# A two-layer graph-attention kernel: projection and gate of layer 0 as one product of fifteen block products

## The chip, the cores and the metric

The kernel runs on one core of one Trainium2 chip. The metric is device time in microseconds (us) for one execution, the median of the runs; the profile is one execution taken by the hardware profiler. TensorE (PE in the profile, its weight loads PEld) multiplies matrices and writes to PSUM, eight banks of 128 x 512 float32. VectorE (DVE), ScalarE (ACT) and GpSimd (POOL) do the elementwise work; SyncE (SP) issues all DMAs of this kernel from one queue.

## The reference

128 graphs of 64 nodes with 768 features go through two layers, each followed by a residual and a layer norm. Cut to what matters:

```python
def _L0_gnn_ref(feat_in, adj, W, b, w_src, w_dst, H_w, H_b):
    h = jnp.einsum('bnd,ade->bane', feat_in, W)          # 12 heads of 64
    th = jnp.tanh(h)
    attn = einsum(th, w_src) + swapaxes(einsum(th, w_dst), 2, 3)
    attn = jnp.where(attn >= 0, attn, 0.2 * attn)
    attn = softmax(jnp.where(~adj, -999.0, attn), axis=-1)
    feat_out = elu(attn @ h + b)
    gate = jax.nn.sigmoid(feat_in @ H_w.T + H_b)
    return gate * feat_out + (1.0 - gate) * feat_in

x = _layernorm(x + _L0_gnn_ref(x, adj, ...))
x = _layernorm(x + _L1_gnn_ref(x, ...))   # q, k, v projections, 6 heads, masked softmax, output projection
```

All arithmetic is in float32. The change lies in layer 0, and in the places of weights that layer 1 finds there.

## The kernel before

A tile is 128 rows (two graphs), a pair is two tiles; there are 32 pairs (`NP`). Layer 0 runs over the pairs one turn after the other, layer 1 then over 16 groups of two pairs. The order of every engine's work is written out by hand (`manual_schedule`), nothing reorders it.

**Block products.** A projection of a pair (256 rows by 768 by 768) is not taken as eight block products of a 2 x 2 split but as seven, in Strassen's manner. `Job` (L247) names them 1 to 7: each is three matmuls (`HK`) of 128 rows by 384 columns (`HALF`), line L270. Four operands are sums of input blocks (`block_sums`, L232), four weight blocks are sums too (`weight_sums`, L213). Products 1, 6, 7 and 4 pile up in one PSUM bank `y`, 2 has a bank `x`, 5 and 3 share `z`; between two products on one bank the partial result is drained: `way_out` (L279) copies it on ScalarE where a result is first written, and adds it on VectorE elsewhere (h: L850 to L852, gate: L866 to L868, values of layer 1: L879 to L881). In each turn three jobs run: `h` and `gate` of pair p, and the values `v` of layer 1 for pair p - 1, whose products 4 and 3 fall in the next turn, under the name `u`. `step` (L305) issues a product and then the drain of the product before it. Layer 1 uses a larger scheme of fifteen products of a 3 x 2 split for q, k and the output (`WIDE`, L70).

**The attention of layer 0**, per tile t (t1 and t0 are the second and the first of a pair): `products` (L884) takes tanh(h) and multiplies it with w_dst on VectorE and w_src on GpSimd; `terms` (L893) reduces both on VectorE into `sd` (128 x 24), writes the first twelve columns, the neighbour terms, to DRAM (`dstd`, L899) and reads them back as rows that all 64 nodes of a graph see (`dd`, L902); `logits` (L922) adds them (L926), `leaky` (ScalarE, L936), `masked` (three VectorE instructions, L942 to L949), `exps` (ScalarE, L955), `probs_by_nodes` (TensorE transposes), `attend` (TensorE, L987), `features` (VectorE L1003 and L1004, ScalarE exponential L1011), `elu1`, `gated` (L1022 to L1029), `stats` and `normed` (layer norm), `by_features` (transposes into `x1T`, operand of the values). `gate_tanh` (ScalarE) and `residual` (GpSimd, L1017) work on the gate.

**The order of a turn.** `TURN` (L121) lists the products; a plan hangs other work behind positions of that list: `at` for pair p, `was` for pair p - 1.

```python
TURN = [
    "h1", "h2", "u4", "u3", "h6", "g1", "h5", "h7", "g2", "g6", "h4",
    "h3", "g5", "g7", "v1", "v2", "g4", "v6", "g3", "v5", "v7",
]
```

In it `terms` of t1 and t0 hang at positions 13 and 14 and `logits` at 16 and 18 of the same turn; `masked` of t1 and t0 at 18 and 20. What lies past the end of the list is carried into the next turn. A DMA that waits for data holds up the DMAs behind it on SP's queue.

Of the kernel before, what the change touches and what calls it, by code (L numbers as in the profile page):

```python
# [24 lines left out]
EP = E0 + 2  # L25
# [21 lines left out]
WOVEN = [  # L47
    (0, 1), (1, 1), (0, 2), (1, 2), (0, 6), (1, 6), (0, 5),
    (0, 7), (1, 5), (1, 7), (0, 4), (0, 3), (1, 4), (1, 3),
]  # L50

FIRST = ["h1", "h2", "h5", "h6", "g1", "h7", "g2", "h4", "g6", "g5", "g7", "h3", "g3"]

FIRST_AT = {3: 0, 6: 10, 8: 3, 11: 8, 12: 12, 13: 12, 14: 13, 15: 14, 16: 14, 17: 14, 18: 15, 19: 19, 20: 19}
SECOND = [
    "h1", "G4", "h2", "g1", "g2", "h6", "h5", "h7", "g6", "h4",
    "g5", "g7", "h3", "g4", "g3", "H1", "v1", "v2", "v6", "v5", "v7", "H2",
]  # L60
SECOND_AT = {11: 10, 12: 13, 13: 13, 14: 14, 15: 14, 16: 15, 17: 16, 18: 18, 19: 19, 20: 20}
SECOND_OLD = {
    7.5: 12, 0: 7, 1: 8, 2: 8, 3: 9, 4: 10, 5: 11, 6: 12, 7: 12, 8: 13, 9: 14, 11: 15, 12: 15, 15: 16, 16: 17, 19: 19,
}

# [26 lines left out]
    ["u4", "u3"]  # L95
    + [f"q{n}" for n in (0, 1, 2, 3, 4, 5, 6, 8, 7, 9, 10, 11, 12)]
    + ["v1", "v2", "v6", "q13", "v5", "v7", "q14", "v4", "v3"]
)
LAST_AT = {7.5: 8, 3: 3, 4: 4, 5: 5, 6: 6, 7: 7, 8: 9, 9: 10, 11: 12, 12: 13, 15: 15, 16: 17, 19: 18}
# [21 lines left out]
TURN = [  # L121
    "h1", "h2", "u4", "u3", "h6", "g1", "h5", "h7", "g2", "g6", "h4",
    "h3", "g5", "g7", "v1", "v2", "g4", "v6", "g3", "v5", "v7",
]

THIRD_AT = {pos: max(int(pos) - 2, 0) for pos in [*range(len(TURN)), 7.5]}
TURNS = {
    0: (FIRST, FIRST_AT, {}),
    1: (SECOND, SECOND_AT, SECOND_OLD),
    2: (TURN[2:], THIRD_AT, THIRD_AT),  # L130
}
# [3 lines left out]
def kernel(  # L135
# [9 lines left out]
    hwT: bass.AP,  # L145
# [33 lines left out]
    dst_d = [dram.tile([P, H0], F32, name=f"dstd_{t}") for t in range(2 * NP)]  # L179
# [199 lines left out]
    def wide_place(key, n):  # L379
        flat = weights[key].rearrange("p b k f -> p (b k f)")  # L380
        at = PLACE[n] * 2 * W2
        return flat[:, at : at + 2 * W2].rearrange("p (k f) -> p k f", k=2)
# [373 lines left out]
    with ExitStack() as ph, ExitStack() as ph_r:  # L756
# [34 lines left out]
        xTs[0] = sbr.tile([P, KC, PAIR * P], F32, tag="xT", name="xT_0")  # L791
        w0_w = weights["q"] = wpool.tile([P, 7, HK, HALF], F32, tag="wa", name="w0_wq")
        for kh, blocks in ((0, (B11,)), (1, (B21, T3, B22))):
            rows = slice(kh * HK, (kh + 1) * HK)
            nc.sync.dma_start(out=xTs[0][:, rows, :], in_=xT[0][:, rows, :])
            for block in blocks:
                load_block(w0, w0_w, block)
        hb_bc = load_rows(sbr, hb, D, "hb_bc")
        b01_bc = load_rows(sb, b0, E0, "b01_bc")
        hw_w = weights["k"] = load_weight(hwT, "wb", "hw_wk", (B11, B21, T3, B22))  # L800
# [3 lines left out]
        A[0], x_steps = sums_of(G, sbr, "sx", xTs[0], "x0")  # L804
        all_of(x_steps)
        t1, t2, t4, t3 = weight_sums(V, w0_w)
        all_of((t1, t2, t3, t4))
# [21 lines left out]
        def new_h(t):  # L829
            h = sb.tile([P, H0, EP], F32, tag="h", name=f"h_{t}", bufs=3)  # L830
            G.memset(h[:, :, E0:], 1.0)
            return h

        h_of = per_tile("h", new_h)
        gate_of = per_tile("gate", lambda t: sb.tile([P, D], F32, tag="gate", name=f"gate_{t}", bufs=3))
        v_of = per_tile("v", lambda t: sb.tile([P, D], F32, tag="v", name=f"v_{t}"))


        def h_job(p):
            def at(m, n):  # L840
                return h_of(p, m)[:, n * J0 : (n + 1) * J0, :E0]

            def as_heads(b):
                return b.rearrange("p (j e) -> p j e", e=E0)

            return token_job(
                f"h{p}",
                A[p],
                w0_w,
                lambda mn, b: S.copy(at(*mn), as_heads(b)),  # L850
                lambda mn, b: V.tensor_tensor(at(*mn), as_heads(b), at(*mn), ALU.add),
                lambda b: S.copy(at(1, 0), as_heads(b)),  # L852
            )

        def gate_job(p):
            def at(m, n):
                return gate_of(p, m)[:, n * HALF : (n + 1) * HALF]

            def bias(n):
                return hb_bc[:, n * HALF : (n + 1) * HALF]  # L860

            return token_job(
                f"g{p}",
                A[p],
                hw_w,
                lambda mn, b: V.tensor_tensor(at(*mn), b, bias(mn[1]), ALU.add),  # L866
                lambda mn, b: V.tensor_tensor(at(*mn), b, at(*mn), ALU.add),
                lambda b: V.tensor_tensor(at(1, 0), b, bias(0), ALU.add),  # L868
            )
# [14 lines left out]
        def products(t):  # L884

            h = st[t]["h"]
            th = sbr.tile([P, 2, D], F32, tag="th", name=f"th_{t}")
            S.activation(th[:, 1, :].rearrange("p (a e) -> p a e", e=E0), h[:, :, :E0], AF.Tanh)
            V.tensor_tensor(th[:, 0, :], th[:, 1, :], wsd[:, 0, :], ALU.mult)  # L889
            G.tensor_tensor(th[:, 1, :], th[:, 1, :], wsd[:, 1, :], ALU.mult)  # L890
            st[t]["th"] = th

        def terms(t):  # L893

            th = st[t].pop("th")
            sd = small.tile([P, 2 * H0], F32, tag="sd", name=f"sd_{t}")
            V.tensor_reduce(sd, th.rearrange("p s (a e) -> p (s a) e", e=E0), AX.X, ALU.add)
            st[t]["sd"] = sd
            nc.sync.dma_start(out=dst_d[t], in_=sd[:, :H0])  # L899
            dd = work(f"dd_{t}")  # L900
            for g in range(2):
                nc.sync.dma_start(  # L902
                    out=dd[g * N : (g + 1) * N, :],
                    in_=dst_d[t][g * N : (g + 1) * N, :]
                    .rearrange("m a -> (m a)")
                    .partition_broadcast(N),
                )
            st[t]["dd"] = dd

        def with_bias(t):  # L910

            h = st[t]["h"]
# [9 lines left out]
        def logits(t):  # L922
# [5 lines left out]
                dd.rearrange("p (m a) -> p a m", a=H0),  # L928
                sd[:, H0:].unsqueeze(2).to_broadcast([P, H0, N]),
# [50 lines left out]
        def attend(t):  # L980
            pT, h, hx = st[t].pop("pT"), st[t].pop("h"), st[t].pop("hx")
# [32 lines left out]
        def residual(t):  # L1014

            xp = st[t]["x"]
            G.tensor_tensor(xp, st[t]["gate"], xp, ALU.mult)  # L1017
# [6 lines left out]
        def gated(t):  # L1024

            ex, gate, u = (st[t].pop(k) for k in ("ex", "gate", "x"))
            V.scalar_tensor_tensor(ex, gate, 4.0, ex, ALU.add, ALU.mult)
# [35 lines left out]

        def gate_tanh(t):

            gt = st[t]["gate"]
# [19 lines left out]
        def x_sums(p):  # L1086
            operands, steps = sums_of(G, sbr, "sx", xTs[p], f"x{p}")
            all_of(steps)
            A.setdefault(p, {}).update(operands)

        def third_begins():
            x = xTs[2]
            A[2] = {1: x[:, :HK, :P], 2: x[:, HK:, :P]}
            jobs["H"] = h_job(2)

# [10 lines left out]
        v_sums, carried = {}, {}  # L1106
        summing = sum_weights(sb)
        for p in range(NP + 1):
# [70 lines left out]
            if p == NP:  # L1179
                flush()  # L1180
                for act in plan.pop(0):
                    act()
# [179 lines left out]
```

## Time and profile before

| | |
|---|---|
| runs, us | 2878.41, 2883.49, 2881.39 (median 2881.39) |
| span of the profiled execution, us | 2888.2 |
| PE busy in it | 2840.2 us, 98% |
| DVE busy | 1924.9 us, 67% |
| ACT busy | 1061.2 us, 37% |
| POOL busy | 1303.5 us, 45% |
| mean granted clock of TensorE | 0.998 |

The span runs from the first to the last instruction. A busy share is an average over both layers; a matmul's end in the profile is modelled, so that the distance from start to start says more than the length of one record. Every float32 matmul of 128 rows leaves two records, so a product of three matmuls leaves six. What bounds a stage is read from what waits last in it; idle time of an engine that others wait for little costs nothing.

### The profile page before, as it was taken

The page shows a single profiled execution, that of the slowest core. Times are in us where ns is not written, and L with a number is a line of the kernel's source. Part 1 is how long each engine was busy: PE and PEld are TensorE (multiplying, and loading weights), DVE is VectorE, ACT ScalarE, POOL GpSimd, SP SyncE. Part 2 cuts the span into 40 slices and gives each one's busy share as a digit, 9 for nine tenths or more (in the row PEclk, how much of TensorE's full clock was granted, in tenths as well). Part 3 has the DMA queues.
Part 4 walks back from the last instruction along what each step waited for, and adds up shares of the span by engine and source line. Part 5 has one row for each costly group of instructions (what it writes and reads, how often), then busy time and mean ns, then how long its engine had stood idle before and what let it go on. Part 6 is the DMA issues. An engine that isn't in the chain of part 4 may idle for free.

```text
span 2888.2 us, 47874 instructions
## 1 busy us (share of the span) xinstructions
PE 2840.2 (98%) x18252; PEld 2075.9 (72%) x18252; DVE 1924.9 (67%) x3203; ACT 1061.2 (37%) x1896; POOL 1303.5 (45%) x1253
## 2 busy tenths in 40 slices
PE   8999999999999999999999999999999999999998
PEld 4565556666566666666668888888888888888886
DVE  7888888887888888777763545555544555554556
ACT  2444444444444444444433223333222333322332
POOL 3444445454444544343343445343545443444534
PEclk9999999999999999999999999999999999999999
DMA  5444444444445444333353434432323333233432
GB/s 182 132 154 145 140 150 143 159 148 151 141 142 162 135 155 142 105 116 108 121 195 96 122 91 111 111 92 84 77 79 111 111 104 95 68 84 94 111 88 74
DMA packets 322068, 348.73 MB, mean 121 GB/s; under 512 B 147888, under 2 KB 247216, under 8 KB 321840
## 3 DMA queue, kind: packets, MB, share of 16 engines
q1 hardware_dynamic: 321840, 345.66, 39.7%
q8 instruction: 146, 2.39, 0.4%
q14 instruction: 82, 0.67, 0.1%
HBM read 198.48 MB, written 122.29 MB: 111 GB/s over the span
## 4 chain that ended last, share of the span: by engine, by line
PE 80%; DVE 9%; DMA 4%; ACT 3%; issue 2%; POOL 1%; SPq 1%; POOLq 0%; DVEq 0%; ACTq 0%
PE z_k L447 9%; PE z_o L494 9%; PE z_q L447 8%; PE y_h L270 6%; PE y_g L270 6%; PE y_k L447 6%; PE y_o L494 6%; PE y_q L447 5%; PE y_v L270 5%; PE z_h L270 4%; PE z_v L270 3%; PE z_g L270 2%; PE cp L634 2%; PE sp L550 2%; PE x_g L270 2%
## 5 line engine op out<-in xcount | busy, mean ns | idle before, releaser
L574 ACT ACTIVATE sc<-sc 128x512 f32<-128x512 f32 x48 | 30.7, 639 | 616.9 <-DVE sc L571 616.9
L695 POOL TENSOR_TENSOR y<-y,bf_bc 128x768 f32<-128x768 f32 x64 | 114.7, 1817 | 295.1 <-DMA y<-x1d 265.5
L507 DVE TENSOR_TENSOR y<-y,z_o 128x256 f32<-128x256 f32 x320 | 127.4, 417 | 140.0 <-PE z_o L494 139.9
L494 PE MATMUL z_o<-wf,so 128*128 128x256 f32 x896 | 215.8, 383 | 2.3 <-DVE y L507 1.2
L447 PE MATMUL z_q<-xs,w_wq 128*128 128x256 f32 x896 | 213.5, 381 | 1.0 <-POOL xs L411 0.9
L411 POOL TENSOR_TENSOR so<-ctxT 128x256 f32<-128x256 f32 x224 | 160.5, 737 | 89.8 <-PE y_o L494 44.0
L447 PE MATMUL z_k<-xs,hw_wk 128*128 128x256 f32 x840 | 200.0, 381 | 0.0
L447 PEld LDWEIGHTS z_q<-xs,w_wq 128*128 128x128 f32 x896 | 168.7, 190 | 25.0 <-POOL xs L411 1.3
L494 PEld LDWEIGHTS z_o<-wf,so 128*128 128x128 f32 x896 | 167.2, 190 | 26.9 <-issue 2.0
L322 POOL TENSOR_TENSOR rs_b<-ve_b,minus_half 128x1 f32<-128x1 f32 x64 | 40.5, 632 | 312.7 <-DVE ve_b L320 311.9
L1017 POOL TENSOR_TENSOR x<-gate,x 128x768 f32<-128x768 f32 x64 | 120.1, 1878 | 135.1 <-ACT gate L1068 121.6
L890 POOL TENSOR_TENSOR th<-th,wsd 128x768 f32<-128x768 f32 x64 | 118.0, 1844 | 137.7 <-DVE th L889 137.7
L447 PEld LDWEIGHTS z_k<-xs,hw_wk 128*128 128x128 f32 x840 | 160.3, 191 | 22.1
L322 POOL TENSOR_TENSOR rs_a<-ve_a,minus_half 128x1 f32<-128x1 f32 x64 | 35.9, 562 | 307.3 <-DVE ve_a L320 307.3
L411 POOL TENSOR_TENSOR xs<-r,r 128x512 f32<-128x512 f32 x112 | 147.8, 1338 | 39.5 <-DMA r<-x1Td 22.5
L462 DVE TENSOR_TENSOR qT<-qT,z_q 128x512 f32<-128x512 f32 x96 | 65.9, 687 | 140.8 <-PE z_q L447 140.8
L270 PE MATMUL y_h<-w_wq,xT 128*128 128x384 f32 x384 | 136.5, 492 | 8.3 <-DMA w_wq<-in_w_dram 7.7
L462 DVE TENSOR_TENSOR kT<-kT,z_k 128x512 f32<-128x512 f32 x96 | 66.0, 687 | 114.9 <-PE z_k L447 112.9
L270 PE MATMUL z_v<-wv,sv_v 128*128 128x384 f32 x384 | 137.5, 494 | 1.0 <-DVE v L880 1.0
L270 PE MATMUL y_v<-wv,x1T 128*128 128x384 f32 x384 | 136.5, 492 | 1.2 <-ACT v L879 0.9
L270 PE MATMUL z_h<-w_wq,sx_x 128*128 128x384 f32 x384 | 137.5, 494 | 0.0
L270 PE MATMUL y_v<-wv,sv_v 128*128 128x384 f32 x384 | 134.9, 488 | 1.9 <-DVE sv_v L241 1.0
(165 smaller groups left out, 6907.7 us busy)
## 6 DMA issues: line engine op xcount, KB each, us to landing
x<-in_x_dram SPq DMA_DIRECT2D x64, 384.0 KB, 3.7
dd<-dstd SPq DMA_DIRECT2D x128, 192.0 KB, 3.4
x1d<-x SPq DMA_DIRECT2D x64, 384.0 KB, 2.6
x1Td<-x1T SPq DMA_DIRECT2D x32, 768.0 KB, 4.5
vd<-v SPq DMA_DIRECT2D x64, 384.0 KB, 2.9
r<-x1Td SPq DMA_DIRECT2D x96, 256.0 KB, 3.4
v<-vd SPq DMA_DIRECT2D x384, 64.0 KB, 2.3
y<-x1d SPq DMA_DIRECT2D x64, 384.0 KB, 5.7
```

The lines of the kernel that those rows point to most:

```text
L270: T.matmul(to[:, : self.n], lhsT, rhs, start=kc == 0 and not more, stop=kc == HK - 1, skip_group_check=more,)
L322: G.tensor_tensor(rstd, ve, minus_half, ALU.pow)
L411: G.tensor_tensor(t, self.of(x[0]), self.of(x[2]), x[1])
L447: T.matmul(b[:, half * W2 : (half + 1) * W2], w[:, kc, half * P : (half + 1) * P], x[:, kc, :], start=half == kc == 0 and not more, stop=k ...
L462: V.tensor_tensor(at, at, b.rearrange("p (h t) -> p h t", h=2), ALU.add if sign > 0 else ALU.subtract,)
L494: T.matmul(b[:, :W2], x[:, kc, :], w[:, kc, :], start=kc == 0 and not more, stop=kc == 1, skip_group_check=more,)
L507: V.tensor_tensor(at, at, self.banks[path][:, :W2], ALU.add if sign > 0 else ALU.subtract)
L550: T.matmul(self.sp_[gr * N : (gr + 1) * N, (i * 2 + a) * N : (i * 2 + a + 1) * N], qT[:, 2 * self.f + a, at], kT[:, 2 * self.f + a, at], s ...
L634: T.matmul(self.cp_[a][e, at], self.v_[rows, i, gr, e], self.scT_[rows, at], start=True, stop=True,)
L695: G.tensor_tensor(y, y, pools["bf"], ALU.add)
L890: G.tensor_tensor(th[:, 1, :], th[:, 1, :], wsd[:, 1, :], ALU.mult)
L1017: G.tensor_tensor(xp, st[t]["gate"], xp, ALU.mult)
```

## The change

- The weights of h and gate lie side by side as one matrix of 768 x 1536 (`wa`, fifteen blocks of 256 x 512), and both results as one tile `hg` of 24 groups of 64 columns. The two jobs of seven products become one job `Fifteen` of fifteen products `a0` to `a14` on a 3 x 2 split: two matmuls of 512 columns each. Products share five banks: 0 on one, 1 on a second, 2 and 4 on a third, 5 and 7 on a fourth, 8, 10, 12 and 14 on a fifth, and 3, 6, 9, 11, 13 on the bank of 0.
- Ten operands are sums of input blocks (`x_sums`, all on GpSimd but for the first pair's), nine weight blocks are loaded, and 17 VectorE sums and one ScalarE negation make the fifteen of them.
- Drains: six copies on ScalarE and ten adds on VectorE a pair, each of 512 columns. The gate's bias is no longer in its drain but added by GpSimd (`gate_bias`).
- Five of seven value products of a pair fall in the next turn (`u6 u5 u7 u4 u3`) and two (`v1 v2`) in its own.
- `logits`, `leaky`, `masked` and `exps` of tile 0 move into the next turn, positions 2 to 4; `probs_by_nodes`, `attend` and what follows move with them.
- `terms` turns `sd` (now 32 columns) on VectorE in 32 x 32 blocks and writes the neighbour terms head by head, in two DMAs for each graph of 12 rows of 32; `dd` and `logits` then read them contiguously.
- The weights of q and k of layer 1 are loaded into the places of `wa` in the order in which the last pair's products free them.

The diff, cut to its core:

```diff
+TURN = "u6 a0 u5 a1 u7 a5 u4 a3 u3 a8 a6 a7 a2 a10 a9 a12 a4 a14 a11 v1 a13 v2".split()
...
+        class Fifteen:
+            def product(self, n):
+                path = PRODUCTS[n][0]
+                more = path in self.banks
+                if not more:
+                    tag = "y" if path in (0, 2) else "z"
+                    self.banks[path] = bank(tag, f"{tag}_a{self.p}_{n}", 3)
+                b, x = self.banks[path], A[self.p][n]
+                for kc in range(2):
+                    T.matmul(b, x[:, kc, :], wa[:, n, kc, :], start=kc == 0 and not more, stop=kc == 1, ...)
+            def way_out(self, n):
+                path, _, reads = PRODUCTS[n]
+                b = as_heads(self.banks[path])
+                for f, t, sign in reads:
+                    f = (0, 2, 1)[f]
+                    at = hg_of(self.p, t)[:, 8 * f : 8 * f + 8, :E0]
+                    if (f, t) in self.written:
+                        V.tensor_tensor(at, at, b, ALU.add if sign > 0 else ALU.subtract)
+                    elif sign > 0:
+                        S.copy(at, b)
+                    else:
+                        S.mul(at, b, -1.0)
...
-            sd = small.tile([P, 2 * H0], F32, tag="sd", name=f"sd_{t}")
-            V.tensor_reduce(sd, th.rearrange("p s (a e) -> p (s a) e", e=E0), AX.X, ALU.add)
+            sd = small.tile([P, 32], F32, tag="sd", name=f"sd_{t}", bufs=2)
+            G.memset(sd[:, 2 * H0 :], 0.0)
+            V.tensor_reduce(
+                sd[:, : 2 * H0], th.rearrange("p s (a e) -> p (s a) e", e=E0), AX.X, ALU.add
+            )
             st[t]["sd"] = sd
-            nc.sync.dma_start(out=dst_d[t], in_=sd[:, :H0])
+            sdT = small.tile([P, 32], F32, tag="sdT", name=f"sdT_{t}", bufs=1)
+            V.transpose(sdT, sd)
             dd = work(f"dd_{t}")
             for g in range(2):
+                for c in range(2):
+                    at = g * N + 32 * c
+                    nc.sync.dma_start(
+                        out=dst_d[t][g, :, 32 * c : 32 * c + 32], in_=sdT[at : at + H0, :]
+                    )
                 nc.sync.dma_start(
                     out=dd[g * N : (g + 1) * N, :],
...
+                was(1, do(probs_by_nodes, t1), do(gate_tanh, t1))
+                was(2, do(residual, t1), do(logits, t0))
+                was(3, do(attend, t1), do(leaky, t0), do(masked, t0))
+                was(4, do(exps, t0), do(features, t1))
+                was(5, do(elu1, t1), do(gated, t1), do(gate_tanh, t0))
+                was(6, do(residual, t0), do(stats, t1))
+                was(7, do(normed, t1), do(probs_by_nodes, t0))
+                was(9, do(by_features, t1), do(attend, t0))
+                was(10, do(features, t0))
+                was(11, do(elu1, t0))
+                was(11.5, do(gated, t0))
+                was(12, do(stats, t0))
...
+            h1, h0 = (1, 5, 6, 3, 7, 8), (4, 9, 0, 14)
+            behind_of(h1, 1, do(products, n1))
+            behind_of(h1, 3, do(terms, n1), do(with_bias, n1))
+            behind_of(h1, 7, do(logits, n1))
+            behind_of(h1, 8, do(leaky, n1))
+            behind_of(h1, 9, do(masked, n1))
+            behind_of(h1, 10, do(exps, n1))
+            behind_of(h0, 1, do(products, n0))
+            behind_of((11,), 1, do(gate_bias, n0))
+            behind_of(h0, 3, do(terms, n0), do(with_bias, n0))
+            behind_of((13,), 1, do(gate_bias, n1))
```

`behind_of(ns, lag, ...)` hangs work `lag` positions behind the last of the products `ns`. In the steady turn (from the fifth pair on) a7 stands at position 11 and a14 at 17, so that `terms` of tile 1 comes at 14 and its `logits` at 18, `masked` of tile 1 and then `terms` of tile 0 at 20, and the `logits` of tile 0 at position 2 of the next turn. The first four turns have lists of their own (`EARLY`).

## The prediction, as it was put on record

> **What bounds the kernel now.** I read the page first (busy shares, the slices, the chain that ended last), then busy time over whole turns, then the order of time inside one turn, then the groups by shape.
>
> ```profile
> PE 2840.2 (98%) x18252; PEld 2075.9 (72%) x18252; DVE 1924.9 (67%) x3203; ACT 1061.2 (37%) x1896; POOL 1303.5 (45%) x1253
> ...
> PE   8999999999999999999999999999999999999998
> ...
> DVE  7888888887888888777763545555544555554556
> ...
> PE 80%; DVE 9%; DMA 4%; ACT 3%; issue 2%; POOL 1%; SPq 1%; POOLq 0%; DVEq 0%; ACTq 0%
> ```
>
> TensorE is full in nearly every slice and carries 80% of the chain; VectorE is second, fuller in layer 0 (the first half) than later. The change touches layer 0 alone. Busy time there, from one start of a value job to the next, and over eight such turns:
>
> ```profile
> 632.64:678.31 45.67, 45.57 (x248) 27.77 (x246) 37.89 (x55) 19.99 (x32) 21.56 (x22) 1.00 0.47 145
> ...
> 632.64:1000.59 367.95, 365.32 (x1970) 221.78 (x1969) 300.49 (x433) 159.90 (x256) 175.83 (x162) 1.00 0.46 148
> ```
>
> Columns: stretch, PE, PEld, DVE, ACT, POOL, clock, DMA. A turn is 367.95 / 8 = 46.0 us, with DVE 37.6, ACT 20.0, POOL 22.0 busy. Matmul ends are modelled, so I use starts: products (six records) follow each other every 1.935 us, and 21 of them are 40.6 us of the 46.0. So TensorE sets the time, almost without a stall. Why it can do so shows in order of time:
>
> ```profile
> 631.36 1.74 DVE L897 TENSOR_REDUCE sd<-th 128x24 f32<-128x1536 f32 x1
> ...
> 633.12 0.33 SPq L899 DMA_DIRECT2D dstd<-sd  x1
> ...
> 634.62 1.11 SPq L902 DMA_DIRECT2D dd<-dstd  x2
> ...
> 639.02 1.52 DVE L926 TENSOR_TENSOR att<-dd,sd 128x768 f32<-128x768 f32 x1 [0.37 <-DMA dd<-dstd]
> ```
>
> The neighbour terms leave VectorE at 633.10 and are back, over DRAM, at 639.02: a round trip of 5.9 us. SP waits 1.5 us for the write before it issues the two reads. VectorE filled the trip with other work and waited 0.37 us.
>
> **What the Trainium skill says.** "TensorE: Matmul & The Clock Gate", section "Architectural detail: the array is 16× 32×32, not 1× 128×128": ScalarE and VectorE queues are strict FIFO, so what stands behind a waiting instruction waits too. The trace agrees: no record of DVE or ACT overtakes. "DMA: Bandwidth & Descriptors", "Two DMAs through the same engine are not ordered": a read of what a DMA wrote must wait for its semaphore. It agrees: the 1.5 us above. "SBUF — State Buffer", "Who interferes with whom": a VectorE instruction with two SBUF inputs and a GpSimd instruction that reads SBUF exclude each other. It agrees: usually 0.96, L1022 takes 1.82 beside L1017:
>
> ```profile
> 610.61 1.81 POOL L1017 TENSOR_TENSOR x<-gate,x 128x768 f32<-128x768 f32 x1
> 611.41 1.82 DVE L1022 SCALAR_TENSOR_TENSOR ex<-ex,fo 128x768 f32<-128x768 f32 x1 [0.54 <-ACT ex L1011]
> ```
>
> "TensorE: Matmul & The Clock Gate", "What's actually happening": after an idle window of about 3.4 us the array runs at half clock until it has been busy as long. After a gap here the next product needed 4.21 us, not 1.94:
>
> ```profile
> 80.00:90.00 10.00, 6.85 (x16) 4.14 (x17) 8.46 (x9) 4.83 (x8) 9.92 (x8) 0.66 0.41 132
> ...
> 84.69 4.21 PE L270 MATMUL y_v<-wv,x1T 128*128 128x384 f32 x6 [0.29 <-ACT x1T L967]
> ```
>
> **The change part by part.** Products. Fourteen products of 3 x 384 columns become fifteen of 2 x 512. No 512-column matmul is in the trace; by columns (256 and 384 both scale so) one product is 1.935 x 1024 / 1152 = 1.72 us. 14 x 1.935 = 27.1, 15 x 1.72 = 25.8: 1.3 us a turn, 42 us over 32 pairs, and a turn of 44.7 if nothing waits.
>
> VectorE. Ten drains of 384 (0.55) become ten of 512, priced by the row L462:
>
> ```profile
> L462 DVE TENSOR_TENSOR kT<-kT,z_k 128x512 f32<-128x512 f32 x96 | 66.0, 687 | 114.9 <-PE z_k L447 112.9 <-ACT scT L623 2.1
> ...
> L926 DVE TENSOR_TENSOR att<-dd,sd 128x768 f32<-128x768 f32 x64 | 109.6, 1713 | 24.7 <-DMA dd<-dstd 24.1
> ```
>
> That is +1.4. The logits read dd contiguously: 1.71 falls to 0.96, the usual time of such an add, twice: -1.5. Two transposes of 128x32 are not in the trace: between 0.15 (the 128x1 TENSOR_SCALAR rows) and 0.31 (the skill's price of a larger one, "VectorE: DVE Perf Modes", "The three transpose paths"); I take 0.15. In sum 37.8, 85% of 44.7. ACT has 6 drains for 4: +1.7, hidden.
>
> GpSimd. Ten sums of 0.737 (the 128x256 row of L411) for four of about 1.0, two gate biases of 1.82, small memsets: +7.2, so 29 of 44.7. It is not the bound, but excludes VectorE more often: 0 to 2 us a turn, part of which is in the walk below.
>
> SP. The write of the terms becomes four (12 partitions x 32), in the order write, write, read, write, write, read, and each read waits for its two writes. From the transpose: second write issued at 0.33, landed 1.5 later (1.8), read issued to 2.4, writes to 3.1, landed 4.3, read, landed 3.75 after its start (as before: 635.18 to about 638.95): 8.1 us. With the fastest landings seen (1.4 and 3.1) it is 7.1, with the median write of 1.9 it is 8.9.
>
> Order. I number the 22 positions of the steady turn from 0 (u6) and start a clock where TensorE ends tile 0's attention, behind a8 at position 9. VectorE then runs in this order: features 1.47, (ScalarE's exponential 0.94), ELU, gate and difference 2.88, drain of a7 0.69, statistics 1.35, product with w_dst 0.96, shift 0.2, drain of a10 0.69, reduction 1.74, transpose 0.15: 12.1, and 0.7 for hand-overs: 12.8. (a12, on the bank of a10 with one product between, waits 1.35 here.) Tile 1's trip: 20.9. Behind its logits stand, on VectorE, tile 0's product and the drain of a11: 0.96 + 0.96 + 0.69, 23.5; a13 accumulates on a11's bank and waits. TensorE alone would be there at 6 x 1.72 + 0.65 + 3 x 1.72 + 1.94 = 18.1: 5.4 us late. Then tile 1's mask and maximum, 1.08 + 0.95 + 0.96, stand ahead of tile 0's reduction and transpose: 28.4. Tile 0's trip: 36.5. Now logits 0.96, leaky 0.84, mask 2.99, and behind them tile 1's features 1.47 and exponential 0.94; on ScalarE the copy that empties u7's bank, 0.48, stands behind that exponential. With hops 44.3, and u4, which accumulates on u7's bank, starts then. From u4 to the end of tile 0's attention TensorE needs 1.94 + 1.72 + 1.94 + 1.72 + 2 x 0.65 + 0.86 = 9.5: 53.8. That is the turn: 7.8 us more than 46.0.
>
> The rest. First product: whole xT, then five vector sums of 0.42, so at 10 to 11 us where 7.67 stood: +3, bounds 0 and +20 (17 weight sums of 1.2 us on VectorE are in that path). Four early turns have another order; there I count only the 1.3 gained: -5, bounds -6 and +20. The loads of layer 1's weights find their places free as products end: 0, within 6.
>
> Sum: 28 x 7.8 = 218, +3, -5: 2888.2 + 216 = 3104 of its own execution's span, which stands 6.8 above the median of the runs; so 3098.
>
> **The rivals.** (1) Not slower: the trips are covered. It is one mechanism, at u4: unstalled, tile 0's reduction ends 5.1 us after a13 starts, u4 is due 16.15 us after it, and 7.8 us follow the trip, so the trip may be 3.3 us; up to 4.6 the turn is no longer than before. Then 28 to 32 turns save up to 1.3: 2842. For it: 12 packets of 128 B a write instead of 128 of 48 B. Against: the read alone never landed under 3.1. (2) Slower by less: the trip stays about 5.9 (the second pair of writes lands under the first read). 53.8 - 2 x 2.2 = 49.4, 28 x 3.4 - 2: 2974. For it: dd's median of 3.4. (3) Slower by more: gaps of 3 to 5 us at a13 and u4 drop the clock, +2.2 a turn as at 84.69: 3159. For it: that place. Against: an idle window must fit wholly into the gap.
>
> **How the numbers follow.** Forecast 0.46, (2) 0.22, (3) 0.18, (1) 0.12, within 0.2% 0.02 (0.2%, 6 us, is what a measurement can tell from no change). Slower is 0.86. The range takes in (2) and (3) and the bounds on the trip (2 x 1 us x 28 = 56): 2930 to 3195; it leaves out (1), no change, and tails of 0.06.
>
> **What would show it.** u4 waiting for ScalarE by 4 to 5 us a turn and a13 for VectorE by 3 to 4; DVE logits waiting for dd over 100 us in total (24.1 before); a trip of 7 to 9 us; turns of 51 to 56 us; products of 1.72. Wrong would be turns of 45 us, or a trip under 5.

## The result, and the profile after

The changed kernel takes 3313.4 us (median of four runs, 3310.2 to 3315.6) where the kernel before takes 2881.6: the ratio is 1.149, 95% interval 1.148 to 1.151. 3098 was forecast: the direction was right, the loss (432 us) is twice the one forecast (216).

First the page of the changed kernel: busy times, the slices of TensorE, of VectorE and of the granted clock, and the chain that ended last.

```profile
PE 2961.5 (89%) x17484; PEld 1988.3 (60%) x17484; DVE 1994.1 (60%) x3282; ACT 1109.6 (34%) x1961; POOL 1532.0 (46%) x1567
...
PE   6858888888888888888888799999999999999998
...
DVE  6846666666666766666666544555555555555556
...
PEclk8989989899898999989899899999999999999999
...
PE 41%; DVE 1%; ACT 0%; DMA 0%; issue 0%; POOL 0%; SPq 0%; POOLq 0%; DVEq 0%; ACTq 0%
```

Layer 0 now takes 23 slices and not 20 of a longer span, and in all of them TensorE and VectorE both have idle time: neither is full, so a wait between them sets the time. The second half is as before. The chain's shares add up to 43%, nearly all lines of layer 1: it was not followed back into layer 0, and says nothing of it. Two whole turns (columns as before: stretch, PE, PEld, DVE, ACT, POOL, clock, DMA) and three groups of layer 0 (busy, mean ns, idle before and its releaser):

```profile
800.74:860.50 59.76, 50.20 (x226) 25.16 (x222) 36.19 (x56) 21.55 (x34) 32.74 (x33) 0.91 0.38 124
860.50:919.23 58.73, 50.05 (x226) 25.17 (x222) 38.99 (x56) 21.56 (x34) 29.15 (x29) 0.91 0.34 109
```

```profile
L896 PE MATMUL y_a<-wa,sx 128*128 128x512 f32 x1024 | 546.9, 667 | 188.4 <-DVE hg L912 160.8
...
L279 PE MATMUL y_v<-wv,x1T 128*128 128x384 f32 x384 | 181.1, 622 | 86.5 <-ACT v L927 86.5
L981 DVE TENSOR_TENSOR att<-dd,sd 128x768 f32<-128x768 f32 x64 | 74.6, 1165 | 289.8 <-DMA dd<-dstd 289.8
```

TensorE waits for VectorE's drain, for the most part ahead of a12 and a13 (160.8 us), and for ScalarE's copy ahead of u4 (86.5); VectorE waits 289.8 us for the neighbour terms, 24.1 before. The first of these turns in order of time, one engine after the other (VectorE, SP, TensorE):

```profile
813.99 0.21 DVE L951 STREAM_TRANSPOSE sdT<-sd 128x32 f32<-128x32 f32 x1 [0.44 <-DMA wided_k<-wacc_k]
...
823.19 0.96 DVE L981 TENSOR_TENSOR att<-dd,sd 128x768 f32<-128x768 f32 x1 [5.18 <-DMA dd<-dstd]
...
830.90 0.21 DVE L951 STREAM_TRANSPOSE sdT<-sd 128x32 f32<-128x32 f32 x1 [0.65 <-POOL sd L945]
...
839.38 0.96 DVE L981 TENSOR_TENSOR att<-dd,sd 128x768 f32<-128x768 f32 x1 [5.46 <-DMA dd<-dstd]
```

```profile
814.23 1.02 SPq L956 DMA_DIRECT2D dstd<-sdT  x2
816.23 0.47 SPq L959 DMA_DIRECT2D dd<-dstd  x1
816.74 0.95 SPq L956 DMA_DIRECT2D dstd<-sdT  x2
819.63 0.47 SPq L959 DMA_DIRECT2D dd<-dstd  x1
```

```profile
825.76 3.53 PE L896 MATMUL y_a<-wa,sx 128*128 128x512 f32 x4 [4.83 <-DVE hg L912]
...
847.09 4.21 PE L279 MATMUL y_v<-wv,x1T 128*128 128x384 f32 x6 [3.07 <-ACT v L927]
851.09 2.99 PE L896 MATMUL y_a<-wa,sx 128*128 128x512 f32 x4
```

From the transpose's end (814.20) to the logits (823.19) is a trip of 9.0 us, the second one (831.11 to 839.38) 8.3. VectorE stands idle for 5.2 and 5.5 us of them, with a drain and a mask behind the waiting logits, and a13 and u4 come late. Behind both gaps the matmuls are at about half clock: counted from start to start, a13 takes 3.3 us for 1.72, u4 4.0 for 1.94 and a3 2.8 for 1.72.

To compare kernels I take the mean steady turn, from the start of VectorE's reduction for tile 1 in the fifth turn to that in the last, divided by 27. Before: (1454.5 - 218.1) / 27 = 45.8 us. After: (1862.4 - 287.2) / 27 = 58.3. Of the 423 us between the spans (3311.2 and 2888.2), 27 x 12.5 = 339 are steady turns, 287.2 - 218.1 = 69 the start and the four early turns, and 15 what comes behind the last of these reductions.

### The profile page after: what moved, and what is told of

It reads as the page before. It is cut to its first block, busy times and chain, and to the rows that moved or that the text cites. A ratio compares the mean times of both kernels' runs of the same rounds, so it can differ in the third digit from the quotient of the medians.

```text
span 3311.2 us, 46975 instructions
## 1 busy us (share of the span) xinstructions
PE 2961.5 (89%) x17484; PEld 1988.3 (60%) x17484; DVE 1994.1 (60%) x3282; ACT 1109.6 (34%) x1961; POOL 1532.0 (46%) x1567
## 3 DMA queue, kind: packets, MB, share of 16 engines
q1 hardware_dynamic: 316720, 345.47, 33.6%
## 5 line engine op out<-in xcount | busy, mean ns | idle before, releaser
L896 PE MATMUL y_a<-wa,sx 128*128 128x512 f32 x1024 | 546.9, 667 | 188.4 <-DVE hg L912 160.8
L896 PEld LDWEIGHTS y_a<-wa,sx 128*128 128x128 f32 x1024 | 207.9, 212 | 444.3 <-issue 314.8
L279 PE MATMUL y_v<-wv,x1T 128*128 128x384 f32 x384 | 181.1, 622 | 86.5 <-ACT v L927 86.5
L981 DVE TENSOR_TENSOR att<-dd,sd 128x768 f32<-128x768 f32 x64 | 74.6, 1165 | 289.8 <-DMA dd<-dstd 289.8
L1072 POOL TENSOR_TENSOR x<-hg,x 128x768 f32<-128x768 f32 x64 | 125.8, 1966 | 226.9 <-ACT hg L1129 226.9
L460 PE MATMUL z_q<-xs,wa 128*128 128x256 f32 x896 | 213.8, 382 | 2.5 <-ACT qT L485 2.5
L460 PE MATMUL z_k<-xs,wa 128*128 128x256 f32 x840 | 198.5, 379 | 0.0
L912 DVE TENSOR_TENSOR hg<-hg,y_a 128x512 f32<-128x512 f32 x224 | 151.8, 678 | 77.5 <-PE y_a L896 59.8
L279 PEld LDWEIGHTS y_v<-wv,x1T 128*128 128x128 f32 x384 | 88.1, 238 | 174.2 <-ACT v L927 109.7
L460 PEld LDWEIGHTS z_q<-xs,wa 128*128 128x128 f32 x896 | 169.2, 190 | 26.6 <-POOL xs L424 2.9
L896 PE MATMUL z_a<-wa,xT 128*128 128x512 f32 x384 | 181.8, 596 | 0.0
L460 PEld LDWEIGHTS z_k<-xs,wa 128*128 128x128 f32 x840 | 159.5, 190 | 21.7
```

Of the source, the lines that this page charges most:

```text
L279: T.matmul(to[:, : self.n], lhsT, rhs, start=kc == 0 and not more, stop=kc == HK - 1, skip_group_check=more,)
L460: T.matmul(b[:, half * W2 : (half + 1) * W2], w[:, kc, half * P : (half + 1) * P], x[:, kc, :], start=half == kc == 0 and not more, stop=k ...
L896: T.matmul(b, x[:, kc, :], wa[:, n, kc, :], start=kc == 0 and not more, stop=kc == 1, skip_group_check=more,)
L912: V.tensor_tensor(at, at, b, ALU.add if sign > 0 else ALU.subtract)
L981: V.tensor_tensor(att3, dd.rearrange("p (a m) -> p a m", m=N), sd[:, H0 : 2 * H0].unsqueeze(2).to_broadcast([P, H0, N]), ALU.add,)
L1072: G.tensor_tensor(xp, gate_of(t), xp, ALU.mult)
```

## The experiments

Each ran beside the kernel before (2880 to 2888 us); two later ones were timed in rounds and have an interval, the others are one run each.

**e1_trip_as_before.** Does the trip of the terms cost the time? Tile 1's logits wait for it, and so do those of tile 0.

```diff
-            V.transpose(sdT, sd)
...
-                for c in range(2):
-                    nc.sync.dma_start(out=dst_d[t][g, :, 32*c : 32*c+32], in_=sdT[at : at + H0, :])
+            nc.sync.dma_start(out=dst_d[t], in_=sd[:, :H0])
```

> The changed kernel with the neighbour terms as before: one DMA of 128 x 12 for the write, two reads, strided logits, no transpose and no GpSimd memset of sd. Theory T1 (the two DRAM trips stand in VectorE's queue and in the chain to a13 and u4): the trips fall from 9.0 and 8.3 us to about 6.2, the transposes and the wait for the memset go (-1.0), the logits cost 0.56 more each (+1.1): about 4.6 us a turn, and [...]the half-clock products go too (-3.2): turns of about 52 us, in all about 3095 us. Rival T3 (the 512-column products, their banks and GpSimd's extra work make the turn long, the trips are covered): no fall, 3313 within 30.

3182.3 us, mean turn 54.1. The trip is 6.7 and 5.6 us in one turn (5.9 and 5.8 on the average of the 27 steady turns, for 8.5 and 8.5 in the changed kernel), and VectorE's waits for it fall, in the stretch from 300 to 1700 us, from 224.4 to 101.0. The rival falls as far as the trips go; the theory is right in kind and gets little more than half of the gain it named: 131 us of 218.

**e4_writes_first.** The same trip with its two graphs not one behind the other on SP:

```diff
             for g in range(2):
                 for c in range(2):
                     nc.sync.dma_start(out=dst_d[t][g, :, ...], in_=sdT[at : at + H0, :])
+            for g in range(2):
                 nc.sync.dma_start(out=dd[g * N : (g + 1) * N, :], in_=dst_d[t][g]...)
```

> The changed kernel with the four writes of the neighbour terms ahead of the two reads, so that SP waits once and not twice. T1: the trip falls by about 1.5 us to 7.0 to 7.5, twice a turn: 3 us, and up to 2 more[...]: 3170 to 3235 us. T3: 3313 within 15.

3172.8 us, mean turn 53.7: at the lower edge of what was expected, with a trip that fell further than expected. SP's queue and VectorE of this run:

```profile
818.02 1.53 SPq L956 DMA_DIRECT2D dstd<-sdT  x4
819.75 1.27 SPq L960 DMA_DIRECT2D dd<-dstd  x2
```

```profile
817.78 0.21 DVE L951 STREAM_TRANSPOSE sdT<-sd 128x32 f32<-128x32 f32 x1
824.09 0.96 DVE L982 TENSOR_TENSOR att<-dd,sd 128x768 f32<-128x768 f32 x1 [2.04 <-DMA dd<-dstd]
```

Four writes and both reads are out 3.0 us after the first issue (818.02 to 821.02), where the changed kernel needed 5.9 (814.23 to 820.10). The trip is 6.1 us, the second one 6.3. Where the second pair of writes stands in the queue is worth 141 us.

**e7_no_trip.** What would be left if the trip cost nothing?

```diff
-            dd = work(f"dd_{t}")
-            for g in range(2):
...
-                dd.rearrange("p (a m) -> p a m", m=N),
+                sd[:, :H0].unsqueeze(2).to_broadcast([P, H0, N]),
```

> The changed kernel without the trip: the terms are still reduced and transposed, but neither written nor read back, and the logits take the node's own neighbour term in place of the neighbours'. Six small DMAs a tile are left out, and so is that part of the computation. Theory (both trips stand in the cycle, 5.2 + 5.5 us of VectorE's waits a turn, and the half clock follows from them): turns of 45 to 48 us, 2930 to 3020, I say 2960. Rival (tile 0's attention, which the order puts late, is the bound by itself): turns of 53 us or more, 3170 or more.

3036.3 us, mean turn 49.3. Neither bound was right: without the trip 9.0 of the 12.5 us a turn are gone, and 3.5 stay. (With the trip its six DMAs a tile leave SP's queue too, and the loads behind them come earlier; how much of the 9.0 that is was not measured.) TensorE's waits from 300 to 1700 us:

```profile
PE y_a L896 <- DVE hg L912: 36.5, 34, 1.7
PE y_v L279 <- ACT v L927: 27.4, 26, 2.1
PE x1Tp L1009 <- ACT pT L1010: 23.7, 27, 1.3
PE av L1030 <- ACT x1T L1010: 8.8, 28, 0.3
```

Even with no trip at all the new order makes TensorE wait at four places: ahead of a12 (1.2 us a steady turn), of u4 (1.0), of tile 1's transposes to features (0.9) and of tile 0's attention (0.3).

**e2_u7_drain_first.** u4 waits because the copy that empties its bank stands on ScalarE behind tile 1's exponential. Put it ahead:

```diff
-                was(4, do(exps, t0), do(features, t1))
+                was(5, do(exps, t0), do(features, t1))
```

> The changed kernel with exps of tile 0 and features of tile 1 hung at position 5, so that on ScalarE u7's copy stands ahead of the exponentials. T1: u4 no longer waits (3.1 us) and runs at full clock (2 to 3 us); tile 1's norm then comes 1 to 2 us late for its transposes: turns shorter by 4 to 6 us, 3140 to 3200 us in all. T3: nothing changes, 3313 within 15.

3362.3 us: slower by 49. TensorE's waits from 300 to 1700 us:

```profile
PE y_a L896 <- DVE hg L912: 120.4, 46, 5.2
PE x1Tp L1021 <- ACT pT L1022: 102.5, 23, 5.8
```

u4's 76.2 us are gone from the list, and 102.5 us stand at tile 1's transposes to features, which are not in the list of the changed kernel. The wait moved along the chain. On the average of the steady turns u4 starts 4.1 us behind tile 0's logits and no longer 8.2, but the first product behind tile 0's attention still starts 20.2 us behind them (20.3 in the changed kernel): features and norm of tile 1 do not come earlier when TensorE does.

The loss itself stands behind that place. The first product there follows the moved gap and is slow, and VectorE needs its drain ahead of tile 0's ELU (TensorE, then VectorE, in one turn):

```profile
883.97 2.73 PE L896 MATMUL y_a<-wa,sx 128*128 128x512 f32 x4
886.54 1.88 PE L896 MATMUL z_a<-wa,xT 128*128 128x512 f32 x4
```

```profile
886.74 0.69 DVE L912 TENSOR_TENSOR hg<-hg,y_a 128x512 f32<-128x512 f32 x1 [1.35 <-PE y_a L896]
```

On the average that product takes 3.2 us from its start to the next (1.8 in the changed kernel), and VectorE waits for TensorE's products 2.0 us in this stretch of a turn and not 0.5: 27 x 1.5 = 40 of the 49 us. Here a slow product costs time.

**e3_filler and e13_filler_whole_gap.** Does the half clock lengthen the turn? Products that belong to nothing, into drained banks, keep TensorE busy in the gaps:

```diff
+                    for pos, path, n in ((6, 3, 2), (20, 4, 3)):     # e13: 4 and 6
+                        if i == new_at[p] + pos:
+                            for _ in range(n):
+                                T.matmul(jobs["a", p].banks[path], A[p][1][:, 0, :], wa[:, 1, 0, :], ...)
```

> The changed kernel with two more 512-column matmuls before u4 and three before a13, into banks already drained, that nothing reads: TensorE is busy in part of the two gaps, and idle for about 1.4 and 2.2 us in one piece. T2 (a gap [...]halves the clock for what follows, and at u4 that lies on the chain): u4 takes 1.94 us again where it took 4.0, a3 1.72 where it took 2.8: about 3 us a turn, 3220 to 3240 us, clock above 0.97. Without T2 (the slow products have another cause): no gain, 3311 to 3340.

> The changed kernel with more of the extra products of e3_filler: four matmuls of 512 columns ahead of u4 and six ahead of a13, so that TensorE has work for the whole of both gaps (3.4 and 5.2 us at 0.86 us each); they are not part of the computation. If the half clock after the gaps is worth what the records show (u4 and a3 3.2 us longer, a13 and x_v 2.0 longer), the clock is near 0.99 and the mean turn falls by 3 to 5 us, to 53 to 55.5: 3160 to 3240. Rival (the turn's length is set by the trips and the chain on VectorE, and what TensorE does faster behind a gap is waited for at the next place): the clock near 0.99 all the same and the mean turn within 1.5 of 58.3: 3270 to 3350.

e3: 3324.0 us, clock 0.970, mean turn 58.6: no gain, as was expected without the theory. But the gaps were not closed. a13 runs at full speed in 24 of the 27 steady turns and u4 in only 8: behind a faster a13 TensorE is earlier at u4 and stands there for 3.3 us in most turns. That left the question open, so e13 fills the whole gaps: 3307.1 us, clock 0.986, mean turn 58.0. TensorE of e13:

```profile
823.91 5.31 PE L1286 MATMUL z_a<-wa,xT 128*128 128x512 f32 x12
829.11 1.96 PE L896 MATMUL y_a<-wa,sx 128*128 128x512 f32 x4
...
850.83 2.20 PE L279 MATMUL y_v<-wv,x1T 128*128 128x384 f32 x6 [1.64 <-ACT v L927]
...
860.33 0.93 PE L1021 MATMUL x1Tp<-ident,x 128*128 128x128 f32 x6 [1.27 <-ACT pT L1022]
```

Both places run at full speed, in all 27 steady turns, and the mean turn is 0.3 us shorter, as the rival said: TensorE is earlier behind u4 and waits at tile 1's transposes instead. The extra products themselves hold a13 up by some 0.7 us on the average, but TensorE still waits 1.2 us a turn ahead of u4 behind them. So at these two places the half clock fills time that would for the most part be waited anyway. The 6 us that e13 gains are less than e5 below finds between two runs without a cause.

**e5_store_early.** One wait of the early turns, in the changed kernel, TensorE and then ScalarE and SP:

```profile
249.01 3.94 PE L279 MATMUL y_v<-wv,sv_v 128*128 128x384 f32 x6 [18.95 <-ACT v L927]
```

```profile
248.48 0.48 ACT L927 COPY v<-y_v 128x384 f32<-128x384 f32 x1 [24.75 <-DMA vd<-v]
```

```profile
241.88 0.91 SPq L1142 DMA_DIRECT2D vd<-v  x2
```

The first copy of the next pair's values takes the buffer of an older pair, whose store is hung behind the end of the fourth turn; products and ScalarE stand until it has landed.

```diff
-                put(new_at[p] + (len(EARLY[p]) + 1 if p < len(EARLY) else 11), do(spill_values, p - 2))
+                put(new_at[p] + (len(EARLY[p]) + 1 if p < 3 else 14 if p == 3 else 11), do(spill_values, p - 2))
```

> The changed kernel, but the store of the second pair's values is issued at position 14 of the fourth early turn and not behind it; nothing else. Theory: ScalarE's first copy of the next pair's values waits 24.75 us for that store, whose buffer it takes, and TensorE stands 18.95 us behind it; the store then lands before the copy is due and the time falls by 15 to 20 us: about 3295 beside 3313. Rival (the wait at that place is one of several that end together, the terms' trip stands behind it): less than 6 us, 3307 to 3320.

3309.4 us. At its place the theory held: the fifth turn's reduction starts at 275.3, 11.9 us earlier. But the mean of the steady turns, where nothing was edited, is 58.7 for 58.3, and 27 x 0.3 takes 8 us back. So a difference under some 9 us between two of these runs says nothing of a cause; why the steady turns moved I have not settled.

**e10_zero_once.** e4's kernel, and GpSimd writes the zero columns of `sd` once and not in each tile:

```diff
-            sd = small.tile([P, 32], F32, tag="sd", ...)
-            G.memset(sd[:, 2 * H0 :], 0.0)
+            sd = sds[t % 2]
```

> The run with four writes ahead of the two reads (3173), with one edit more: the zero columns beside the terms are written once at the start and not by GpSimd in each tile, so that VectorE's reduction no longer waits for GpSimd's queue. Theory (VectorE's 0.97 and 0.65 us of waiting for that memset a turn stand in the cycle, where a whole chain over both tiles sets the time): 30 to 50 us less, 3125 to 3145. Rival (the reduction needs GpSimd's product, which ends little earlier than the memset): 3160 to 3180.

3168.3 us, mean turn 53.5, 4 us less than e4, which is no difference: the rival. VectorE's reduction still waits 25.3 us in 1400 us, now named as a wait for GpSimd's product.

**e6_later_order and e8_order_and_trip.** Leave the trip as it is, but put VectorE's other work ahead of the logits that wait for it:

```diff
-            behind_of(h1, 7, do(logits, n1))
-            behind_of(h1, 8, do(leaky, n1))
-            behind_of(h1, 9, do(masked, n1))
-            behind_of(h1, 10, do(exps, n1))
+            behind_of(h1, 10, do(logits, n1))
+            behind_of(h1, 10, do(leaky, n1))
+            behind_of(h1, 11, do(masked, n1))
+            behind_of(h1, 12, do(exps, n1))
...
-                was(2, do(residual, t1), do(logits, t0))
+                was(3, do(residual, t1), do(logits, t0), do(leaky, t0))
```

> The changed kernel with its DMAs and buffers as they are; only the order on VectorE, ScalarE and TensorE's transposes changes: tile 1's logits, leaky, mask and exponential come three positions later, its transposes one, and all of the turn's attention from tile 0's logits on one position later, so that drains and products stand ahead of the logits on VectorE while the trip runs. Theory (the trips cost because they are waited for in VectorE's queue): VectorE waits for dd under 80 us in all instead of 290, turns of 46 to 50 us instead of 58.2, 2960 to 3090, I say 3030. Rival (the wait moves only, as when the drain of u7 was put first; the chain over both attentions is the bound and not the trips): turns of 56 us or more, 3240 or more.

> All three together: the later order, the four writes ahead of the two reads, the store of the values at position 14 of the fourth early turn, and the zero columns beside the terms written once and not by GpSimd in each tile. Theory (then nothing of the trips is left in the cycle, and the products set the turn): turns of 45 to 47 us, VectorE waits for dd under 30 us, 2890 to 2960, I say 2920; near the kernel before, its start and early turns being longer. Rival (order as before is needed as well, with 768 columns of logits and the attention of both tiles ahead of u4): turns of 50 us or more, over 3040.

e6: 3179.8 us, mean turn 53.6: 133 us from the order alone, less than half of what I had said. Its waits for dd are 85.2 us in all, 67.1 from 300 to 1700 us; new ones took their place, 98.5 on TensorE for tile 1's exponential and 80.2 on VectorE for GpSimd's product. Much of what is missing goes with GpSimd's background sums of layer 1's weights: in the last eight turns, where none of them runs, the turn is 49.7 us, in 18 turns with them 55.3; in the changed kernel the two figures are 58.1 and 58.5. No run leaves the sums out, so that they are the cause is not shown. e8, with the writes first, the early store and the zeros: 3073.5 us, mean turn 50.8. Time and turn are above its theory and where its rival had put them, though VectorE's waits for dd are down to 7.7 us in all, as the theory said: what is left is no longer the trips. Two of its waits, on GpSimd and then VectorE:

```profile
836.10 0.73 POOL L375 TENSOR_TENSOR wacc_k<-wacc_k,wadd_k 128x256 f32<-128x256 f32 x1 [3.64 <-DMA wadd_k<-in_wk_dram]
836.78 1.80 POOL L938 TENSOR_TENSOR th<-th,wsd 128x768 f32<-128x768 f32 x1
```

```profile
838.61 1.75 DVE L949 TENSOR_REDUCE sd<-th 128x24 f32<-128x1536 f32 x1 [3.12 <-POOL th L938]
```

A background sum of layer 1's weights waits 3.6 us on GpSimd for its load, tile 0's product with w_src stands behind it, and VectorE's reduction behind that.

**e9_refined_order and e11_best_order.** So the remaining waits were taken one by one. e9's moves, and behind them what e11 adds:

```diff
-TURN = "... a8 a6 a7 a2 a10 a9 a12 ..."
+TURN = "... a8 a6 a7 a10 a2 a9 a12 ..."
...
+                        yield                        # one step more between a load and its sum
...
-                was(8, do(normed, t1), do(probs_by_nodes, t0))
-                was(10, do(by_features, t1), do(attend, t0))
+                was(8, do(probs_by_nodes, t0), do(normed, t1))
+                was(10, do(attend, t0))
+                was(12, do(by_features, t1), do(elu1, t0))
...
-            behind_of(h1, 10, do(logits, n1))
+            behind_of(h1, 8, do(logits, n1))
```

```diff
-                was(2, do(probs_by_nodes, t1))
+                was(3, do(probs_by_nodes, t1))
...
-                was(5, do(exps, t0), do(features, t1))
+                was(5, do(exps, t0), do(attend, t1))
+                was(6, do(features, t1), do(gate_tanh, t0))
...
-                was(16, do(by_features, t0), do(v_begins, q), do(v_sum, q, 0))
+                was(16 if q else 18, do(by_features, t0), do(v_begins, q), do(v_sum, q, 0))
```

> The run of the later order, early writes, early store and zero columns written once (3073), with five more moves within the turn: a10 changes places with a2, so that two products and not one lie between a10 and a12 on its bank; tile 1's logits stand behind a11's drain and ahead of tile 0's terms; tile 1's gate is turned one position earlier; tile 0's transposes and attention stand ahead of tile 1's norm and of its transposes to features; and the background sums of later weights are used one step later after their loads were issued. Theory (what is left of the cost are waits in the FIFO queues: 52 us for the probabilities, 40 for a drain, 27 for pT in 1400 us, and VectorE's 54 for GpSimd's product, which stands behind a sum that waits for its load): turns of 46 to 48 us, 2930 to 3010, I say 2970. Rival (VectorE and GpSimd exclude each other so often with 37.8 and 29 us of work that no order brings the turn under 50): 3050 to 3100.

> The refined order (2954) with three moves more: tile 1's transposes of probabilities, its attention and what follows each one position later, because TensorE still waited 24.5 us for tile 1's exponential in 1200 us; tile 1's norm one later; and, for the first pair alone, tile 0's transposes to features and the value sums two positions later, because TensorE waited 11.2 us for its norm in the third early turn. Theory (the steady turn is then bounded by the products, and what remains against the kernel before are start and early turns, +45 us, less 28 turns of up to 0.8 us saved): 2915 to 2945, I say 2930, still slower than before. Rival (the later tile 1 pushes tile 0's chain and new waits open): 2950 to 2990.

e9: 2953.6 us, mean turn 46.7, as the theory said. e11, timed in rounds: 2945.7 us (2943.3 to 2949.5), 1.021 of the kernel before, interval 1.020 to 1.023; mean turn 46.3. It ends just above its theory (2945), and its 8 us less than e9 are within what two runs differ by. Its page:

```profile
PE 2820.9 (96%) x17484; PEld 1929.9 (65%) x17484; DVE 1981.1 (67%) x3282; ACT 1102.3 (37%) x1961; POOL 1502.9 (51%) x1505
...
PE   7689999999999999999989999999999999999998
```

From the fourth slice on TensorE is nearly full again. The last four turns, in which the background sums are over, are 44.5 us apart (before: 45.4 without the sums): there the fifteen products save 0.9 us of the 1.3 forecast. In the turns with the sums it is 46.5 (before: 46.0), so nothing is saved there. Of the 59 us between the spans (2947.3 and 2888.2), 40 are the start and the early turns (the fifth turn's reduction is at 258.2), 13 the steady turns (27 x 0.5) and 6 the end.

**e12_best_trip_as_before.** e11's order with the edit of e1 in place of the four writes and the zero columns:

> The run with the best order, but with the trip of the terms as the kernel before has it: no transposes on VectorE, one write of 128x12, two reads, logits that read dd with stride (1.71 us for 0.96). Theory (once the trip is covered by the order its length does not matter, and only VectorE's work of 1.5 - 0.4 us a turn differs, which mostly lies beside the products): within 15 us of that run, either way, or up to 30 slower where VectorE is nearly the bound. Rival (the long trips of four writes still cost even here): 15 us or more faster than that run.

2944.8 us (2941.4 to 2947.5), 1.021, interval 1.020 to 1.023: the same time, as the theory said. In this order turning the terms on VectorE is neither gain nor loss. It doesn't show that the length of a covered trip is free: the trips are as long here (6.5 and 6.3 us on the average) as in e11 (6.4 and 6.7), and the trip of 8.5 us was not tried in this order. No version tried beats the kernel before.

## Why the prediction was right in direction and wrong in size

- **Products.** 1.72 us forecast and measured (three products that follow each other start at 802.57, 804.28 and 806.00). A turn of 44.7 if nothing waits: e11's last turns have 44.5. The kernel before has 45.4 there and not 46.0, so the saving is 0.9 and not 1.3.
- **The mechanism.** Trips that stand in VectorE's queue, a13 waiting for VectorE, u4 for ScalarE, the logits for dd: right, in the trace and in e1, e4 and e7. a13 waited 4.8 us in the turn shown and 4.1 on the average of the steady turns (3 to 4 forecast), u4 3.1 and 3.2 (4 to 5).
- **The walk through the turn**, with the clock started at 800.74:

| place | forecast | measured |
|---|---|---|
| tile 1's terms turned | 12.8 | 13.5 |
| a12 waits | 1.35 | 1.37 |
| tile 1's trip back | 20.9 | 22.4 |
| a13 starts | 23.5 | 25.0 |
| tile 0's terms turned | 28.4 | 30.4 |
| tile 0's trip back | 36.5 | 38.6 |
| u4 starts | 44.3 | 46.4 |
| tile 0's attention ends | 53.8 | 59.8 |

The trips were sized at 8.1 and took 9.0 and 8.3; VectorE also waited 1.0 us for GpSimd's product (and the memset right behind it) and 0.65 for a memset that stands on GpSimd behind the gate's bias. Up to u4 the walk is 2.1 us short. One slip made it look better than it was: the terms listed up to the first transpose add up to 11.1 us and not to 12.1. Summed rightly, the walk would have had u4 at 43.3 and the end of the turn at 52.8.

- **The step that failed** is the last: "From u4 to the end of tile 0's attention TensorE needs 1.94 + 1.72 + 1.94 + 1.72 + 2 x 0.65 + 0.86 = 9.5: 53.8. That is the turn". It took 13.4 in the turn shown and 12.1 on the average of the 27 steady turns. I followed TensorE alone there, at full speed. In the turn shown TensorE runs through these 13.4 us almost without a wait, with u4 and a3 at half clock (3.2 us more), which had been set aside as rival (3). But e13 has u4 at full speed in every steady turn, and there the stretch still takes 11.7 us, with 1.3 us of waits at tile 1's transposes and tile 0's attention. Tile 1's features, exponential, ELU, gate, norm and transposes, on VectorE and ScalarE, are the longer branch: in e13 17.2 us from tile 0's logits (843.13) to tile 1's transposes (860.33), and 2.5 more to the product behind tile 0's attention (862.80), 19.7 together (19.5 on the average), where the forecast had 7.8 + 9.5 = 17.3. e2 shows the same branch from the other side: with u4 on time, TensorE waits there.

  By stages, on the average of the steady turns: from the end of tile 0's attention to its next logits 38.0 us (36.5 forecast), on to u4 8.2 (7.8), on to the end of the attention 12.1 (9.5): 58.3 for 53.8. So the last step holds 2.6 of the 4.5 us; 0.8 are in the two trips (8.5 each for 8.1). In sum 216 us were forecast and 423 measured between the spans: of the 207 missing, 121 are in the steady turns (339 for 218), 71 in the start and early turns (69 for -2), 15 behind the last turn's reduction.
- **The early turns.** "Four early turns have another order; there I count only the 1.3 gained: -5", with a bound of +20, and +3 for the first product. Measured +69 up to the fifth turn. The first product was sized well (9.9 us for 7.67), but in the first 290 us TensorE waits 33.6 us for ScalarE's copies of values, most of it because stores free their buffers late (19.0 at the place of e5, 8.8 in the turn before), 19.9 for drains, and 5.8 for summed weights. The step that failed here is the -5: I had not walked these turns. e5 took the longest of these waits away and brought the fifth turn 11.9 us forward; what the others cost is open.
- **Rival (1)**, trips covered, said that a trip of up to 4.6 us would cost nothing. With no trip at all (e7) the turn is 49.3: the threshold came from the same walk, which left out the waits of tile 1's branch.
- **Rival (3)** had a slower clock by 2.2 us a turn. The clock was slower, and by more than that: u4 and a3 alone took 3.2 us longer in the turn shown. Its argument against, that an idle window must fit wholly into the gap, did not hold: gaps from 2.49 us on were enough ahead of u4. e13 shows that at these places the slow clock was not what set the turn; e2 shows a place where it would be.
- **The end.** The loads of layer 1's weights were put at nothing, within 6 us: 15 us are left over behind the last turn's reduction, and their cause was not looked into.

What the theory says now, argued from the walk and in keeping with every run: in a turn of the changed kernel, one chain runs through the attention of both tiles, and through both trips. Shortening the trips (e1, e4), or covering them (e6), gives 4.2 to 4.8 us of the 12.5 each; both with the rest of the order gives 12.0 (e11). Of that sum, what the later attention of tile 0 costs by itself was seen only together with the order around it (the 3.5 us of e7).

## What to carry to other kernels

A round trip over DRAM cost time here because its data were waited for in a FIFO queue with others' work behind: before counting its microseconds, list what waits behind the first instruction that needs its data, and put that ahead. When two tiles hand over to each other on one engine, follow every branch from the last wait to the end of the turn and take the longest; the engine with the most work need not be on it. Slow products behind a gap cost little where the next wait takes up the time (e13), and much of their length where another engine needs the slow product (e2). Walk the first turns separately: buffers that a steady turn finds free may there be held by a store that is issued late.

## What the runs showed of the hardware

- On one DMA queue, write, write, read, write, write, read took 8.3 to 9.0 us from the transpose to the logits that wait for the data; the same six with the four writes first 6.1 to 6.3. The second pair of writes has its data from the start; it stands behind a read that waits for the first pair to land.
- Gaps shorter than the idle window of about 3.4 us that the Trainium skill states ("TensorE: Matmul & The Clock Gate", section "What's actually happening") were enough for slower matmuls. In the changed kernel TensorE stood idle for 2.49 to 4.60 us ahead of u4 in the 27 steady turns, and u4 was slow in every one of them (2.7 to 4.0 us for 1.94). The kernel before has such a place at 84.69, where a product took 4.0 us, behind transposes that waited 3.31 us:

```profile
82.86 1.54 PE L966 MATMUL x1Tp<-ident,x 128*128 128x128 f32 x6 [3.31 <-ACT x L327]
```

  No sharp bound comes out of the runs: in e3, u4 was at full speed behind gaps of up to 3.27 us in eight turns, and a13 was slow behind 2.12, 2.59 and 2.78 us in three.
- A 128 x 768 operation of VectorE can lose more beside GpSimd than the 0.96 to 1.82 us shown above: the subtraction of the maximum took up to 2.42 us in e7 and 2.50 in e9, and the kernel before has 2.40 for its L1029 beside GpSimd's L1017.
